# Source scores and row flags written to DRAM by element, and more steps for turned rows, in a six-layer graph network

## The chip, the core and the metric

The kernel runs on one core of a Trainium2 chip. The metric is device time in microseconds (us) of one execution, from launch to end; lower is better. TensorE multiplies matrices into PSUM, VectorE (DVE), ScalarE (ACT) and GpSimd (POOL) work on tiles of 128 partitions, SyncE (SP) issues most DMA transfers. "Dry" or "stopped" means that TensorE has no matmul that it may start.

## The reference

A graph of N = 3327 nodes with 256 features each and a sparse adjacency matrix `adj` passes four attention blocks; the last consists of three layers, so the kernel has six, called 0, 1, 2, 3a, 3b and 3c. Weights, scales and the handling of nodes without neighbours are left out here:

```python
x = layernorm(x + cos_attention(x, adj))      # 0: softmax over Kn @ Qn.T, rows of norm 1
x = layernorm(x + gat(x, adj, W, a))          # 1
x = layernorm(x + qk_attention(x, adj))       # 2: softmax over q @ k.T / 16, values x @ Wv.T
h = x @ W0                                    # 3a, 3b, 3c
for W, a in three_layers:
    h = gat(h, adj, W, a)
x = layernorm(x + h)

def gat(x, adj, W, a):
    h = x @ W
    e = leaky_relu((h @ a[:256]) + (h @ a[256:]).T)   # one source and one target score per node
    att = softmax(where(adj > 0, e, very_negative), axis=1)
    return elu(att @ h)
```

In layer 0 a node without neighbours keeps its features: its flag is whether its sum of weights is zero.

## The kernel before

**Tiles and blocks.** The nodes are padded to 3328, which makes 26 tiles of 128 sources (index j) and 7 blocks of 512 target nodes (index b; block 6, the last, has 256). One step is a triple (layer, block, tile): it makes a tile of unnormalized attention weights `e`, 128 sources by 512 targets, and multiplies it with the 128 by 257 tile of values (the last column is ones and gives the sum of weights), into accumulators `po` in PSUM. The main loop at the end of `gnn_stack` runs over all 6 × 7 × 26 steps; at step s it calls `make(s + 2)`, so weights are made two steps ahead.

**Weights.** In the three GAT layers and layer 1 (`Gat.weights`), ScalarE makes a relu (L599) from the exponential `u` of the source scores of the block, DVE adds and masks it (L607). `u` is loaded from DRAM by `block` (L586, every partition gets the block's row `s_d`, L591 is the exponential; two buffers), in steps 14 and on of the block before. In layer 2 `weights2` takes two matmuls (L506), an exponential (L514) and the mask (L433); layer 0 is alike (L444, L453, L433). Masks are kept in DRAM as bytes (`mask_d`) and fetched a block ahead by L370, 1.66 MB each, at step 8 of a block in program order.

**Products.** Layers 1, 3a, 3b and 3c use plain matmuls (L1163). Layer 2, and blocks 1 to 5 of layer 0, use Strassen's seven products on pairs of tiles (`products`, L704): the sums of the weights (`sums`, L651 to L654) are made by DVE, the sums of the values (`combine`, L625) once per pair when the values are made; they go to DRAM (`t_d`, L636) and are fetched for each block and pair by `fetch_tsum` (L640 to L643, three buffers).

**After a block.** When a block's 26 tiles are accumulated, a generator `finish(L, b, pos)` is appended to a queue, and the main loop advances it by one `yield` per step; at j = 20 of the next block all that is pending is emitted at once. `finish` normalizes (L878 to L882 free the accumulators), turns the rows (`turn`), projects them (`pproj`, L924), applies elu, in layers 0, 1, 2 and 3c the layer norm (L982), writes rows to `x_d` (L994), and for layer 1 turns the result again and makes the values and keys of layer 2 (`pv`, L1011). `NB` is 7, so `b == NB - 2` is block 5, the last full one, and `NB - 1` the last, of 256.

**Turned rows.** `turn` copies the two 16-bit halves of each number into planes (ScalarE, L759), lets SP issue one DMA transposition of them (L762), yields `steps` times, and copies the halves back with DVE (L769, two copies) for the matmul that follows.

**Scores of the next layer.** `Gat.scores` (L533) makes each node's source and target scores on DVE in `self.sd`, one column per tile. `shift` (L548) takes the largest of them, `keys` (L563) the exponentials of the target scores, and `rows(b)` brings the block's source scores to `s_d`: a TensorE transpose (L577, `psr`), a ScalarE copy (L579) and a DMA of four rows of 128 (L580).

**Row flags.** In layer 0 `z0` is 1.0 where a node's sum is below 0.1. A TensorE transpose (L853, `plone`) and a ScalarE copy to bytes (L855) turn it, the mask goes to DRAM (L856), and the flags go into its last row (L857).

**What sets the order.** The program order above is the order of emission. The scheduler of the language then orders the instructions of each engine, except in the first steps, which are ordered by hand. `po` has five PSUM buffers and a block uses three or four, the other PSUM tiles (`ps`, `pproj`, `pv`, `psr`, `plone`) share three, `e` has five buffers. Each engine, SP too, issues in its order, and an instruction that waits holds up those behind it.

Of the kernel before, what the change touches and what calls it, by code (L numbers as in the profile page):

```python
# [8 lines left out]
F32 = mybir.dt.float32  # L9
I32 = mybir.dt.int32  # L10
U8 = mybir.dt.uint8
# [3 lines left out]
ALU = mybir.AluOpType  # L15
# [4 lines left out]
P = 128  # L20
# [13 lines left out]
def gnn_stack(ctx: ExitStack, tc: tile.TileContext, a: dict, N: int, out: bass.AP):  # L34
# [8 lines left out]
    nc = tc.nc  # L43
    NT = (N + P - 1) // P
    NP = NT * P
    NB = (NP + CH - 1) // CH
# [3 lines left out]
    def bw(b):  # L50
        return min(CH, NP - b * CH)

    def tiles_of(b):
        return range(4 * b, min(4 * b + 4, NT))
# [4 lines left out]
    cols = ctx.enter_context(tc.tile_pool(name="cols", bufs=2))  # L59
# [6 lines left out]
    def bank(name):  # L66
        return ps_b.tile([P, CH], F32, tag="pb", name=name)
# [16 lines left out]
    n = 1  # L84
# [9 lines left out]
    ident = const.tile([P, P], F32, name="ident")  # L94
# [12 lines left out]
    s_d = [dram.tile([1, bw(b)], F32, name=f"s_d{b}") for b in range(NB)]  # L107
# [413 lines left out]
    class Gat:  # L521
# [51 lines left out]
        def rows(self, b):  # L573

            n = len(tiles_of(b))
            pr = bank("psr")
            nc.tensor.transpose(pr[:n, :P], self.sd[:, 0, 4 * b : 4 * b + n], ident)  # L577
            r = cols.tile([4, P], F32, tag="srow", name="srow")
            nc.scalar.copy(r[:n], pr[:n, :P])  # L579
            nc.sync.dma_start(s_d[b].rearrange("o (k p) -> (o k) p", p=P), r[:n])  # L580

        def block(self, b):

# [38 lines left out]
    def strassen(L, b):  # L622
        return L.key == "2" or (L.key == "0" and 0 < b < NB - 1)
# [16 lines left out]
    def fetch_tsum(key, b, p):  # L640
        t = work.tile([P, 4 * H + 1], F32, tag="tsum", name="tsums", bufs=3)
        nc.sync.dma_start(t, t_d[key][p])
        tsums[b, p] = t  # L643
# [105 lines left out]
        return z[:, : 2 * q]  # L749


    def turn(x4, n, out, steps=3):

        half = "p k (n t) -> p t k n"
        pl = work.tile([P, 4, 2, D], U16, tag="x4k", name="planes", bufs=2)
        for t in range(2):
            nc.scalar.copy(pl[:, :n, t, :], x4[:, :n, :].bitcast(U16).rearrange(half, t=2)[:, t])  # L759
        yield  # L760
        tr = work.tile([P, 16, P], U16, tag="stage", name="turned", bufs=3)
        nc.sync.dma_start_transpose(  # L762
            out=tr[:, : 4 * n, :], in_=pl[:, :n].rearrange("p k t n -> p (k t n)")
        )
        for _ in range(steps):
            yield
        trv = tr[:, : 4 * n, :].rearrange("p (k t h) i -> p t k h i", t=2, h=2)
        for t in range(2):
            nc.vector.tensor_copy(out(t), trv[:, t])  # L769
        yield  # L770
# [19 lines left out]
    def finish(L, b, pos):  # L790
# [4 lines left out]
        n = len(ts_)  # L795
# [9 lines left out]
        def follow(ks, vals):  # L805

            for k in ks:

                if b == NB - 2:
                    L.late.append((ts_[k], vals[k]))  # L810
                else:
                    L.sum.add(ts_[k], vals[k])
                if L.gat_next is not None:
                    L.gat_next.scores(ts_[k], vals[k])

        if L.key == "0":
            am = anyadj.pop(b)[:, :n]

            if strassen(L, b):
                y4 = work.tile([P, 4, D], F32, tag="x4k", name="y4", bufs=2)  # L820
                z_ = joined(pos, b, y4)
                nc.vector.tensor_scalar(z_, z_, TINY, None, ALU.max)
            else:
                z_ = cols.tile([P, 4], F32, tag="zc", name="zc")
# [14 lines left out]
                ys.append(y)  # L839
            yield  # L840

            z0 = cols.tile([P, 4], F32, tag="z0", name="z0")
            nc.vector.tensor_scalar(z0[:, :n], z_[:, :n], 0.1, None, ALU.is_lt)
            c2 = cols.tile([P, 4], F32, tag="c2", name="c2")
            nc.vector.tensor_scalar(c2[:, :n], am, -1.0, 2.0, ALU.mult, ALU.add)
            for k, t in enumerate(ts_):
# [2 lines left out]
                )  # L849
                if k % 2:  # L850
                    yield
            pl = bank("plone")
            nc.tensor.transpose(pl[:n, :P], z0[:, :n], ident)  # L853
            lone = cols.tile([4, P], U8, tag="lone", name="lone")
            nc.scalar.copy(lone[:n], pl[:n, :P])  # L855
            nc.sync.dma_start(mask_d[b], masks[b][:, : NT * wd])  # L856
            nc.sync.dma_start(  # L857
                mask_d[b][P - 1 : P, (NT - 1) * wd :].rearrange(
                    "o (k p) -> (o k) p", p=P
                ),  # L860
                lone[:n],
            )
            for k in range(n):
                stats(k)
# [2 lines left out]
        else:  # L867
# [15 lines left out]
            if L.key in x_d:  # L883
                x4 = work.tile([P, 4, D], F32, tag="stage", name="x4", bufs=3)
# [9 lines left out]
            if L.key != "2" and not final:  # L894
                pT4 = work.tile([P, 4, 2, P], F32, tag="x4k", name="pT4", bufs=2)
                yield from turn(
                    p4,
                    n,
                    lambda t: pT4[:, :n].bitcast(U16).rearrange(
                        "p k h (i t) -> p t k h i", t=2  # L900
                    )[:, t],
                    5 if b == NB - 2 else 3,
                )
                pTs = {k: pT4[:, k] for k in range(n)}

# [64 lines left out]
        if not L.hidden:  # L970
            v = cols.tile([P, 4], F32, tag="var", name="var")
            nc.vector.tensor_scalar(v[:, :n], st[:, :n, 1], LN_EPS, None, ALU.add)
            r = cols.tile([P, 4], F32, tag="rstd", name="rstd")
            rsqrt(r[:, :n], v[:, :n], n)
            yield
            if L.key in ("1", "3c"):
                o4 = work.tile([P, 4, D], F32, tag="stage", name="o4", bufs=3)
                dsts = [o4[:, k, :] for k in range(n)]
            else:
                dsts = [nxt[t][:, :D] for t in ts_]  # L980
            for k, t in enumerate(ts_):
                nc.vector.tensor_scalar(  # L982
                    dsts[k],
                    ys[k],
                    st[:, k, 0:1],
                    r[:, k : k + 1],
                    ALU.subtract,
                    ALU.mult,
                )
                if L.key == "3c":  # L990
                    q = LASTP if t == NT - 1 else P
                    nc.sync.dma_start(out[t * P : t * P + q, :], dsts[k][:q])
                elif L.key in ("1", "2"):
                    nc.sync.dma_start(x_d["2" if L.key == "1" else "3c"][t], dsts[k])  # L994
                if k == 1:
                    yield
            if L.key == "3c":
                return
            yield
            if L.key == "1":  # L1000
                yield from turn(
                    o4,
                    n,
                    lambda t: FT[b].bitcast(U16).rearrange(
                        "p h (k i t) -> p t k h i", k=4, t=2
                    )[:, t, :n],
                )
                for k, t in enumerate(ts_):
                    pm = bank("pv")
                    for h in range(2):  # L1010
                        nc.tensor.matmul(  # L1011
                            pm[:, :D],
                            FT[b][:, h, k * P : (k + 1) * P],
                            w["v"][:, h, :],
                            start=(h == 0),
                            stop=(h == 1),
                        )
                    nc.vector.tensor_tensor(nxt[t][:, :D], pm[:, :D], w["bv"], ALU.add)
                    if k % 2:
                        yield  # L1020
                        if b < NB - 1:
                            combine("2", t // 2, nxt)
                dsts = [nxt[t][:, :D] for t in ts_]
            for k in range(0, n, 2):
                follow((k, k + 1), dsts)
                yield
# [24 lines left out]
    class Layer:  # L1051
# [6 lines left out]
    layers = [  # L1058
        Layer(0, "0"),
        Layer(1, "1", gat=True),  # L1060
        Layer(2, "2"),
        Layer(3, "3a", gat=True, hidden=True),
        Layer(4, "3b", gat=True, hidden=True),
        Layer(5, "3c", gat=True),
    ]
# [16 lines left out]

    steps = [(L, b, j) for L in layers for b in range(NB) for j in range(NT)]
    made = deque()

    def make(s):
        if s >= len(steps):
            return
        L, b, j = steps[s]
        if strassen(L, b) and j % 2 == 0:  # L1090
            fetch_tsum(L.key, b, j // 2)
        if L.is_gat:
            made.append(L.gat.weights(b, j))
        else:
            made.append((weights0 if L.key == "0" else weights2)(b, j))
            if strassen(L, b) and j % 2:
                e2, e1 = made.pop(), made.pop()
                made.append(None)
                made.append(sums(b, e1, e2))
# [18 lines left out]
    for s in range(LA):  # L1118
        make(s)
# [4 lines left out]
    for s, (L, b, j) in enumerate(steps):  # L1124
# [25 lines left out]
        if j == 0 and first:  # L1150
            load_x(1)
            load_xT(2)
            make(s + LA)
            next(prep[0])
        elif j == 1 and first:
            make(s + LA)
            next(prep[0])
        else:
            make(s + LA)
# [122 lines left out]
```

## Time and profile before

| | |
|---|---|
| median of 3 runs | 2386.36 us (2385.39 to 2390.31) |
| profiled execution | 2386.53 us |
| its span, first to last instruction | 2384.5 us |
| mean granted TensorE clock | 0.996 |
| psr transposes, plone transposes | 28, 7 |
| DMA transpositions (L762) | 34 |
| fetches of sums (tsums) | 156 |
| loads of masks (L370) | 35 |

The span falls into stages, read off the timeline by the first matmuls of each layer. Columns: from and to in us, length, busy us and instructions of each engine, granted clock, mean busy share of the 16 DMA engines, GB/s.

```profile
0.00:110.00 110.00, 101.02 (x415) 76.06 (x416) 78.61 (x266) 65.91 (x179) 3.79 (x71) 0.97 0.61 193
110.00:486.00 376.00, 372.75 (x2366) 299.70 (x2365) 348.74 (x983) 253.04 (x375) 0.45 (x1) 1.00 0.58 182
486.00:825.00 339.00, 336.46 (x1544) 290.86 (x1543) 226.68 (x576) 186.39 (x286) 7.80 (x12) 1.00 0.30 79
825.00:1412.00 587.00, 585.39 (x3205) 421.88 (x3205) 382.93 (x1144) 160.92 (x278) 0.92 (x4) 1.00 0.24 74
1412.00:1732.00 320.00, 318.49 (x1471) 276.30 (x1471) 192.88 (x460) 186.68 (x296) 0.82 (x2) 1.00 0.18 53
1732.00:2052.00 320.00, 318.07 (x1466) 276.24 (x1465) 189.37 (x439) 185.92 (x293) 0.44 (x1) 1.00 0.18 51
2052.00:2366.00 314.00, 313.41 (x1442) 272.79 (x1440) 189.78 (x451) 174.34 (x270) 0.00 (x0) 1.00 0.20 60
2366.00:2385.00 19.00, 3.02 (x13) 1.84 (x12) 6.52 (x27) 2.52 (x6) 0.00 (x0) 0.71 0.07 23
```

The rows are the start, layers 0 to 3c, and the tail; the engines' columns are PE, PEld (TensorE's loads of weights), DVE, ACT and POOL. A matmul of an fp32 tile is two passes; where two follow each other their modelled ends overlap, so the distance from start to start is what TensorE spends on one: 0.434 us for the 257 columns of a tile of values, against a mean duration of 0.381 us per pass on the page.

### The profile page before, as it was taken

What the parts mean: (1) busy time and instruction counts of PE and PEld (TensorE: products, weight loads), DVE (VectorE), ACT (ScalarE), POOL (GpSimd) and SP (SyncE); (2) the same over time, 40 slices, a digit from 0 to 9 for tenths busy, and PEclk for the clock granted to TensorE, in tenths of its full rate; (3) what the DMA queues carried; (4) which work ended last, traced back from release to release, by engine and by line L of the source; (5) the groups of instructions that cost most, each with busy time, mean ns of one, the idle gap of its engine ahead of it and who ended that gap; (6) DMA issues with size and microseconds to landing.
All of it is one profiled execution on the core that took longest, in us unless ns stands there. A gap on an engine that the chain in (4) does not pass through costs nothing.

```text
span 2384.5 us, 33058 instructions
## 1 busy us (share of the span) xinstructions
PE 2348.6 (98%) x11911; PEld 1915.7 (80%) x11911; DVE 1615.5 (68%) x4340; ACT 1215.7 (51%) x1982; POOL 14.2 (1%) x91
## 2 busy tenths in 40 slices
PE   9999999999999999999999999999999999999997
PEld 6687777888888776667767798888888888888886
DVE  7789999866676657567567585556656555655665
ACT  5666666665555422222222255565655555655554
POOL 0000000000000000000000000000000000000000
PEclk9999999999999999999999999999999999999999
DMA  7556555523222322212212221221211111132121
GB/s 230 169 164 193 187 183 185 164 89 87 73 75 64 102 54 91 73 59 87 72 51 73 78 92 47 67 56 31 73 49 43 43 59 50 45 98 69 60 61 27
DMA packets 146233, 212.83 MB, mean 89 GB/s; under 512 B 76062, under 2 KB 100885, under 8 KB 141461
## 3 DMA queue, kind: packets, MB, share of 16 engines
q1 hardware_dynamic: 145796, 210.45, 29.3%
q8 instruction: 94, 1.54, 0.3%
q14 instruction: 71, 0.57, 0.1%
q10 hardware_dynamic: 272, 0.26, 0.1%
HBM read 165.70 MB, written 28.19 MB: 81 GB/s over the span
## 4 chain that ended last, share of the span: by engine, by line
PE 64%; DVE 2%; DMA 1%; ACT 1%; issue 0%; DVEq 0%; POOL 0%; POOLq 0%; SPq 0%; ACTq 0%
PE po L1163 37%; PE ps L506 12%; PE po L704 11%; PE pproj L924 3%; PE pgq L465 1%; DMA turned<-planes 1%; ACT re L599 1%; DMA t_d<-tsum 0%; PE pv L1011 0%; DVE e L607 0%; DVE ejunk L533 0%; DVE pT L769 0%; ACT planes L759 0%; DMA u<-s_d 0%; DVE v L953 0%
## 5 line engine op out<-in xcount | busy, mean ns | idle before, releaser
L1163 PE MATMUL po<-v,e 128*128 128x257 f32 x5720 | 1275.7, 381 | 2.8 <-ACT p L882 2.0
L1163 PEld LDWEIGHTS po<-v,e 128*128 128x128 f32 x5720 | 1083.2, 190 | 178.1 <-issue 14.6
L599 ACT ACTIVATE re<-u,nrh,th 128x512 f32<-128x512 f32 (+1 forms) x728 | 558.8, 783 | 488.6 <-DVE e L607 485.8
L607 DVE SCALAR_TENSOR_TENSOR e<-re,rh,mask 128x512 f32<-128x512 f32 (+1 forms) x728 | 515.1, 711 | 389.5 <-PE po L1163 366.3
L433 DVE SCALAR_TENSOR_TENSOR e<-ex,mask 128x512 f32<-128x512 f32 (+1 forms) x364 | 236.5, 655 | 183.0 <-ACT ex L514 156.7
L506 PE MATMUL ps<-gT,ft 128*128 128x512 f32 (+1 forms) x728 | 307.7, 563 | 0.0
L514 ACT ACTIVATE ex<-ps,off 128x512 f32<-128x512 f32 (+1 forms) x182 | 119.4, 657 | 360.3 <-PE ps L506 332.3
L704 PE MATMUL po<-tsums,ssum 128*128 128x128 f32 (+1 forms) x1794 | 250.1, 275 | 3.0 <-DMA tsums<-t_d 1.6
L704 PEld LDWEIGHTS po<-tsums,ssum 128*128 128x128 f32 x1794 | 224.4, 192 | 5.4 <-DMA tsums<-t_d 2.4
L704 PEld LDWEIGHTS po<-v,e 128*128 128x128 f32 x1196 | 169.7, 191 | 71.6 <-issue 54.3
L506 PEld LDWEIGHTS ps<-gT,ft 128*128 128x128 f32 x728 | 131.9, 190 | 113.6 <-issue 110.7
L704 PE MATMUL po<-v,e 128*128 128x129 f32 x1196 | 183.2, 275 | 0.2 <-DVE e L433 0.2
L453 ACT ACTIVATE ex<-ps 128x512 f32<-128x512 f32 (+1 forms) x182 | 102.9, 565 | 119.3 <-PE ps L444 107.3
L444 PE MATMUL ps<-ft,ft 128*128 128x512 f32 (+1 forms) x312 | 142.9, 566 | 0.8 <-ACT ft L356 0.7
L405 DVE CUSTOM_DVE_ANT_0 acc<-acc,stage 128x1024 uint16<-128x1024 uint16 (+1 forms) x168 | 111.5, 663 | 13.0 <-DMA stage<-in_adj_a 8.3
L704 PE MATMUL po<-v,ssum 128*128 128x128 f32 x598 | 92.3, 275 | 0.0
L704 PE MATMUL po<-tsums,e 128*128 128x128 f32 x598 | 92.2, 275 | 0.0
L397 ACT ACTIVATE mask<-pos 128x1024 uint8<-128x1024 bf16 (+1 forms) x87 | 86.6, 995 | 2.4
L396 ACT ACTIVATE pos<-stage 128x1024 bf16<-128x1024 int32 (+1 forms) x87 | 85.8, 987 | 2.7 <-DVE e L433 2.7
L924 PE MATMUL pproj<-w_l_w,pT 128*128 128x256 f32 x312 | 80.2, 381 | 3.8 <-DVE pT L769 2.2
L704 PEld LDWEIGHTS po<-v,ssum 128*128 128x128 f32 x598 | 79.4, 192 | 0.1
L704 PEld LDWEIGHTS po<-tsums,e 128*128 128x128 f32 x598 | 79.3, 192 | 0.1
(191 smaller groups left out, 1667.9 us busy)
## 6 DMA issues: line engine op xcount, KB each, us to landing
mask<-mask_d SPq DMA_DIRECT2D x30, 1664.0 KB
tsums<-t_d SPq DMA_DIRECT2D x156, 256.5 KB
stage<-in_adj_a SPq DMA_DIRECT2D x78, 512.0 KB
mask_d<-mask SPq DMA_DIRECT2D x6, 1664.0 KB
t_d<-tsum SPq DMA_DIRECT2D x26, 256.5 KB
u<-s_d SPq DMA_DIRECT2D x24, 256.0 KB
mask<-mask_d SPq DMA_DIRECT2D x5, 832.0 KB
v<-in_x SPq DMA_DIRECT2D x26, 128.0 KB
```

Source lines behind the costliest of these rows:

```text
L397: nc.scalar.activation(mask(b, j, 2), t_[:, : 2 * wd], AF.Sign)
L405: nc.vector.tensor_tensor(acc, acc, st[:, h * wd : (h + 1) * wd], ALU.add)
L433: nc.vector.scalar_tensor_tensor(e[:, :wd], t_[:, :wd], 0.0, mask(b, j), ALU.add, ALU.mult)
L444: nc.tensor.matmul(ps[:, :wd], FT[j // 4][:, 0, (j % 4) * P : (j % 4 + 1) * P], FT[b][:, 1, :wd], start=True, stop=True,)
L453: nc.scalar.activation(t_[:, :wd], ps[:, :wd], AF.Exp)
L506: nc.tensor.matmul(ps[:, :wd], FT[j // 4][:, h, (j % 4) * P : (j % 4 + 1) * P], g[:, h, :wd], start=(h == 0), stop=(h == 1),)
L514: nc.scalar.activation(t_[:, :wd], ps[:, :wd], AF.Exp, bias=off, scale=1.0 / D**0.5)
L599: nc.scalar.activation(t_[:, :wd], self.u[b][:, :wd], AF.Relu, bias=self.nrh[:, j : j + 1], scale=self.th[:, j : j + 1],)
L607: nc.vector.scalar_tensor_tensor(e[:, :wd], t_[:, :wd], self.rh[:, j : j + 1], mask(b, j), ALU.add, ALU.mult,)
L704: nc.tensor.matmul(o, x, y, start=(p == 0 and g not in banks[:i]), stop=(p == NT // 2 - 1 and g not in banks[i + 1 :]),)
L924: nc.tensor.matmul(pm[:, :D], pT[:, h, :], w[L.w][:, h, :], start=(h == 0), stop=(h == 1),)
L1163: nc.tensor.matmul(pos[k], es[:, k * P : (k + 1) * P], V[L.i % 2][j], start=(j == 0), stop=(j == NT - 1),)
```

## The change

Four things are changed.

- `rows` issues one DMA that writes the block's columns of `self.sd` to `s_d` with the partition as the running index of DRAM: 128 × 4 elements of four bytes. Transpose and copy are gone.
- In layer 0 DVE writes the flags as bytes, and the DMA into the mask's last row takes them in the same manner, 128 × 4 elements of one byte. Transpose, copy and the fp32 tile are gone.
- `turn` yields 4 times between the transposition and the copies in place of 3; the projection's turn 7 in place of 5 for block 5; the turn of layer 1's output 6 in place of 3 for block 5.
- `make` fetches the sums of a pair one pair earlier, except for pair 12 of layer 2's first block.

```diff
@@ rows @@
             n = len(tiles_of(b))
-            pr = bank("psr")
-            nc.tensor.transpose(pr[:n, :P], self.sd[:, 0, 4 * b : 4 * b + n], ident)
-            r = cols.tile([4, P], F32, tag="srow", name="srow")
-            nc.scalar.copy(r[:n], pr[:n, :P])
-            nc.sync.dma_start(s_d[b].rearrange("o (k p) -> (o k) p", p=P), r[:n])
+            nc.sync.dma_start(
+                s_d[b].rearrange("o (k p) -> (o p) k", p=P),
+                self.sd[:, 0, 4 * b : 4 * b + n],
+            )
@@ turn @@
-    def turn(x4, n, out, steps=3):
+    def turn(x4, n, out, steps=4):
@@ finish, layer 0 @@
-            z0 = cols.tile([P, 4], F32, tag="z0", name="z0")
-            nc.vector.tensor_scalar(z0[:, :n], z_[:, :n], 0.1, None, ALU.is_lt)
+            lone = cols.tile([P, 4], U8, tag="lone", name="lone")
+            nc.vector.tensor_scalar(lone[:, :n], z_[:, :n], 0.1, None, ALU.is_lt)
...
-            pl = bank("plone")
-            nc.tensor.transpose(pl[:n, :P], z0[:, :n], ident)
-            lone = cols.tile([4, P], U8, tag="lone", name="lone")
-            nc.scalar.copy(lone[:n], pl[:n, :P])
             nc.sync.dma_start(mask_d[b], masks[b][:, : NT * wd])
             nc.sync.dma_start(
                 mask_d[b][P - 1 : P, (NT - 1) * wd :].rearrange(
-                    "o (k p) -> (o k) p", p=P
+                    "o (k p) -> (o p) k", p=P
                 ),
-                lone[:n],
+                lone[:, :n],
             )
@@ finish, projection's turn @@
-                    5 if b == NB - 2 else 3,
+                    7 if b == NB - 2 else 4,
@@ finish, turn of layer 1's output @@
+                    6 if b == NB - 2 else 4,
@@ make @@
-        if strassen(L, b) and j % 2 == 0:
-            fetch_tsum(L.key, b, j // 2)
+        if j % 2 == 0:
+            for n in (s, s + 2):
+                if n < len(steps) and not (n > s and steps[n] == (layers[2], 0, NT - 2)):
+                    if strassen(*steps[n][:2]) and n not in fetched:
+                        fetch_tsum(steps[n][0].key, steps[n][1], steps[n][2] // 2)
+                        fetched.add(n)
```

More of the change, by code (lines that the diff above doesn't have):

```diff
@@ L1084, in gnn_stack @@
     made = deque()
+    fetched = set()
     def make(s):
```

## The prediction

> **What bounds the kernel now.** I read the page's busy times first, then the chain, then TensorE's list of waits, then the timeline at the boundaries of the layers.
>
> ```profile
> span 2384.5 us, 33058 instructions
> ...
> PE 2348.6 (98%) x11911; PEld 1915.7 (80%) x11911; DVE 1615.5 (68%) x4340; ACT 1215.7 (51%) x1982; POOL 14.2 (1%) x91
> ...
> q1 hardware_dynamic: 145796, 210.45, 29.3%
> ...
> PE po L1163 37%; PE ps L506 12%; PE po L704 11%; PE pproj L924 3%; PE pgq L465 1%; DMA turned<-planes 1%; ACT re L599 1%; DMA t_d<-tsum 0%; PE pv L1011 0%; DVE e L607 0%; DVE ejunk L533 0%; DVE pT L769 0%; ACT planes L759 0%; DMA u<-s_d 0%; DVE v L953 0%
> ```
>
> TensorE is the bound: busy 98% of the span and, by line, nearly all of the chain. So only two kinds of edit move the time: work taken off TensorE, and a longer or shorter stop of TensorE. All SP transfers share one queue, q1, with room on average (29.3%).
>
> The list of waits says what TensorE's stops are (total us, times, longest):
>
> ```profile
> PE pproj L924 <- DVE pT L769: 3.1, 6, 0.7
> ...
> PE po L1163 <- ACT p L882: 2.0, 2, 1.3
> PE po L704 <- DMA tsums<-t_d: 1.6, 1, 1.6
> ...
> PE psr L577 <- DVE sd L533: 1.1, 1, 1.1
> ...
> PE pv L1011 <- DVE ft L769: 1.0, 1, 1.0
> ...
> PE pn L488 <- DVE g L485: 0.5, 1, 0.5
> ```
>
> These are the stops that the change can touch; together they are under 10 us. The tile table of psr counts the transposes, and the timeline shows the end of layer 1 (start, duration, engine, line) and the one long stop early in the kernel:
>
> ```profile
> L577 PE MATMUL psr<-ident,sd x28: 269/272/273, 151.7 to 2070.6; 128*4 128x128 f32 x24, 128*2 128x128 f32 x4
> ```
> ```profile
> 816.54 1.94 SPq L762 DMA_TRANSPOSE turned<-planes  x1
> ...
> 816.80 4.58 PE L1163 MATMUL po<-v,e 128*128 128x257 f32 x20
> ...
> 819.16 0.36 SPq L370 DMA_DIRECT2D mask<-mask_d  x1
> ...
> 820.87 1.36 DVE L769 COPY ft<-turned 128x1024 uint16<-128x1024 uint16 x2 [0.51 <-DMA turned<-planes]
> ...
> 822.37 3.69 PE L1011 MATMUL pv<-w_l_wvt,ft 128*128 128x256 f32 x16 [0.99 <-DVE ft L769]
> ```
> ```profile
> 101.91 1.12 PE L352 MATMUL pqkT<-ident,qk 128*128 128x128 f32 x4 [3.31 <-DVE qk L346]
> ```
> ```profile
> 100.00:101.00 1.00, 0.00 (x0) 0.00 (x0) 0.90 (x5) 0.00 (x0) 0.00 (x0) 0.80 0.87 332
> 101.00:102.00 1.00, 0.09 (x1) 0.10 (x1) 0.93 (x6) 0.43 (x2) 0.00 (x0) 0.50 0.44 158
> ```
>
> The last two lines are slices of 1 us; the number after ACT's and POOL's is the granted clock. After a stop of 3.31 us it falls to 0.50. The mean clocks of the slices 95 to 102 (0.90) and 102 to 110 us (0.66) give 1.4 and 5.4 us at half rate, 6.8 in all, which costs half of that, 3.4 us.
>
> **What the Trainium skill says.** "TensorE: Matmul & The Clock Gate" (Part 1: The HAM clock gate) says that TensorE falls to half rate after an idle window of about 3.4 us, a free-running one, and needs about 3.4 us of work to come back; the trace agrees in kind (3.31 us, then 6.8 us at half). "DMA: Bandwidth & Descriptors" (Rules for kernel authors) says that a strided last dimension lowers to one descriptor per element; no such write is in the trace of before. The same page (Bandwidth) has 10.5 ns of busy time per small packet; the trace's 4-byte and 16-byte packets took 9 ns. Its section on queues and rings says that each ring is consumed in order, which makes what stands ahead in SP's queue matter.
>
> **The change part by part**, on the profiled execution, 2386.53 us (span 2384.5 and 2.03 around it), which lies 0.17 above the median, 2386.36.
>
> *Transposes.* 28 psr and 7 plone leave TensorE. A row says 272 ns, but with its overlap the next matmul starts 0.11 us after (psr at 463.36, next at 463.46): 35 × 0.11 = 3.9 us. In 110–486 us, where 13 of them stand, DVE is busy for 349 of 376 us and might swallow their 1.4; elsewhere nothing does. I take −3.9, range −2.5 to −3.9. ScalarE's 35 copies (28 × 256, 7 × 239 ns, 8.8 us) cost nothing now: ScalarE is at 51%. The psr stop at 463.36 (1.1 idle) goes, but DVE's scores, 8 L533 rows, hold up the next weights there: −0.5 (0 to −1.1).
>
> *Element-wise writes.* 28 of 512 (4 of them 256) 4-byte elements, and 7 of one-byte ones, all on q1. Low: 512/16 × 9 ns = 0.3 us. High: read-modify-write at ten times that, 3 us a write. s_d is read a block or a layer later, mask_d a layer later, so either is hidden. In layer 2 the load u<-s_d and a sum's fetch stand behind such a write; a pair of steps is 6.56 us and fetches run up to two pairs ahead, so 3 us fits. I take 0, up to +1. If that cover were gone, each of the writes beyond it would show in full.
>
> *Sums one pair earlier.* SP still waits for the buffer (three of them) that the products L704 release; it did so at 138 fetches, 491 us in all, so the order on SP hardly moves: 0. The exempted pair 12 of layer 2's first block has the 1.6 us stop on tsums; it stays.
>
> *More steps for turned rows.* From L762 to the first copy takes 4.3 us (816.54 to 820.87) to 5.3 (742.72 to 748.02), the two copies 1.36. Ordinary turns get one step more, four matmuls of 0.434 us, 1.7: their stops (0.32 at 749.43, 0.28 at 1612.81; 0.48 and 0.45 by the starts of the matmuls) go: −0.9. The turns of the last-but-one block (about 0.75 each, four times) get two steps more for the copies, but in the built order the first projection stands where it stood: 0 (0 to −1.5).
>
> *Ends of 3a and 3b.* The two steps more push shift, L548, from the 18th to the 20th tile of the last block and so the second exp of u (L591, it waits for a DMA, 0.67 us) behind the copies L882 that free the accumulators. L882 then comes earlier; the stops of 0.63 and 1.32 (0.80 and 1.49 by starts) mostly go: −1.8 (0 to −2.3). Late next is the weights' work on DVE, which has 2.5 us.
>
> *End of layer 1.* Here steps are added at the wrong place. Block 5's output turn gets 3 steps more and its projection turn 2, but at j=20 of the next block all that is pending is emitted at once. In the built order the normalization L982 comes behind the last weights e (L607 of tile 25), and then planes, L762, copies, pv L1011. In SP's queue the next mask's load L370 (1.66 MB, which waits for the last e) and four rows of x (L994) now stand ahead of L762, where L370 stood behind it before. Let T be the end of tile 20's matmuls. Ten matmuls × 0.434 = 4.3 us are left, so TensorE is dry at T+4.3. DVE has o4 at about T+2.3, ScalarE's two planes (1.99) end at T+4.3: the transposition is only then issued. It takes 4.3 to 5.3, copies 1.36, and up to some us for what is left of the mask (8 packets an engine × 498 ns = 4.0 us, most of it done by then) and x (1.5 us). Stop: 4.6 + 1.4 + 1.0 = 7.0 us, ends 5.7 and 9.6. Before, the stops at pv and pn were 1.7 (1.16 and 0.68 by starts, less rounding): +5.3 (4.0 to 7.9). A stop beyond 3.31 us brings the half clock: +3.4, as measured at 101 us (1.7 to 3.4). Nothing in layer 2 makes this up: pv stands ahead of ps L506 on TensorE. What follows the turn moves with it, the sums' t_d writes L636 among it, but their pairs are fetched some 60 us into layer 2 (ten pairs of 6.56 us).
>
> Sum: −3.9 −0.5 −0.9 −1.8 = −7.1; +5.3 +3.4 = +8.7; net +1.6, so 2388.1 on the profile, 2388.0 on the median. Ends of this case: gains of 4.0 to 7.6, losses of 5.7 to 11.3, so −1.9 to +7.3; the middle of that with opposite ends rarely meeting is 2384.5 to 2392.
>
> **The rivals.**
> *The stop at the end of layer 1 stays hidden* (0.16): the chip runs ScalarE's planes early enough that L762 is issued 3 us sooner, as DVE's idle gaps in that stretch allow. The stop is then 3.3 or less and keeps the clock: +1.5, net −5.6, 2380.8. For it: the built order fixes only the sequence, not the times. Against: L982 behind the last e.
> *Slower: the mask's load delays the transposition* (0.36). If its packets take the 926 ns of their 90th percentile, 7.4 us a load, 3.7 are still ahead of the turn when it is issued, and x's 1.5: stop 4.8 + 1.36 + 5.2 = 11.4, +9.7, clock +3.4, gains −7.1: +6.0, 2392.4. It decides from a stop of about 10.2 us with all gains, or 7 with gains of 3.9. For it: ring order; against: at 29% the queue drains.
> *Element writes show* (0.03 of the slower cases): at 0.3 us a packet, 9.6 us a write, 3 beyond the 6.6 of a pair in layer 2's seven: +21, 2409.
> *The change doesn't do what it says*: for the sums' fetches this I take as likely (0 above); for the transposes it can't be.
>
> **How the numbers follow.** Within 0.2% means ±4.8 us (2381.6 to 2391.1), about what a measurement of this kernel tells from no change. Forecast case 0.48: nearly all of it lies within. Hidden stop 0.16: faster. Mask 0.33 and element writes 0.03: slower, the latter far out. So faster 0.17 with the forecast's low tail, same 0.46, slower 0.37. The time is the forecast's, 2388.0; the range takes in the hidden stop to 2380 and the mask's delay with its upper end, 2396.5.
>
> **What would show it.** 5983 TensorE instructions in place of 6018, no psr or plone. At the end of layer 1 pv L1011 with an idle of 6 to 10 us <-DVE ft L769, and a slice of clock 0.5 after it. No stop at L924 in ordinary blocks, still 0.7 at the last-but-one's. po L1163 <- ACT p L882 under 0.5 in all. The tsums' 1.6 unchanged. I am wrong if pv's idle is under 3 us, or if u<-s_d or tsums stop TensorE in layer 2.

## The result and the profile after

The changed kernel takes 2534.94 us (median of 5 runs, 2531.90 to 2535.43) against 2386.81 us of the kernel before beside it (5 runs): a ratio of 1.0616, 95% interval 1.0601 to 1.0632, or +148 us. The prediction, 2388.0 us with a range to 2396.5, is far off.

The page of the changed kernel, lines as those shown of before:

```profile
span 2529.7 us, 32926 instructions
...
PE 2372.8 (94%) x11876; PEld 1937.5 (77%) x11876; DVE 1613.8 (64%) x4340; ACT 1204.4 (48%) x1947; POOL 12.9 (1%) x91
...
PEclk9988988888999999999999999999999999999999
...
q1 hardware_dynamic: 162736, 210.45, 35.5%
```

The span grew by 145.2 us. TensorE's idle time went from 35.9 (2384.5 - 2348.6) to 156.9 us, +121.0; its busy time grew by 24.2 although 35 transposes are gone. The clock's row says why: in seven of the slices 3 to 10 the granted clock is 0.8, since TensorE comes out of its long stops at half rate (the last column but two in the slices below). All but two of TensorE's new stops over 2 us lie in the first 640 us, in layer 0 and at the start of layer 1.

The list of TensorE's waits of the changed kernel (total us, times, longest):

```profile
PE po L703 <- DMA tsums<-t_d: 45.2, 6, 15.4
PE po L703 <- issue: 30.4, 4, 11.9
PE po L1166 <- DVE e L433: 27.5, 2, 20.1
PE pv L1007 <- DVE ft L768: 9.2, 1, 9.2
...
PE pproj L919 <- DVE pT L768: 4.4, 5, 1.7
...
PE po L1166 <- ACT p L877: 1.5, 3, 0.6
```

The fourth line is the stop that was predicted. The first three were not. In the first and the third, layer 0 waits for loads from DRAM: of the sums directly (four of the six times; the other two, 4.0 and 1.1 us, are in layer 2), and of adjacency stages, for which DVE waits ahead of e. For the four stops of the second line the profile names no releaser; they end 16 to 28 us after a write of flags was issued. The DMA engines show what happens in slices around one of the first line's stops. Columns as in the table of stages: granted clock, DMA share and GB/s at the end.

```profile
214.00:217.00 3.00, 3.00 (x26) 2.78 (x25) 3.00 (x11) 2.71 (x5) 0.00 (x0) 1.00 0.66 168
217.00:222.00 5.00, 5.00 (x36) 4.04 (x35) 4.81 (x14) 4.73 (x9) 0.00 (x0) 1.00 1.14 41
222.00:227.00 5.00, 5.00 (x36) 4.04 (x35) 5.00 (x19) 3.20 (x4) 0.00 (x0) 1.00 1.04 38
227.00:232.00 5.00, 2.58 (x12) 1.43 (x11) 5.00 (x19) 1.19 (x2) 0.00 (x0) 1.00 0.99 23
232.00:237.00 5.00, 0.00 (x0) 0.00 (x0) 3.45 (x15) 0.00 (x0) 0.00 (x0) 0.67 0.87 19
237.00:243.00 6.00, 0.00 (x0) 0.00 (x0) 0.00 (x0) 0.00 (x0) 0.00 (x0) 0.50 0.69 52
243.00:247.00 4.00, 1.99 (x9) 2.02 (x10) 0.69 (x1) 2.11 (x2) 0.00 (x0) 0.50 0.89 317
```

The flags of a block are written at 214.13 us (the timeline of SP and of TensorE):

```profile
214.13 0.37 SPq L852 DMA_DIRECT2D mask_d<-lone  x1
```
```profile
228.75 0.83 PE L703 MATMUL po<-v,e 128*128 128x129 f32 x6
245.01 2.04 PE L703 MATMUL po<-tsums,ssum 128*128 128x128 f32 x8 [15.43 <-DMA tsums<-t_d]
```

From 217 to 237 us the DMA engines are busy for about all of their time and move 19 to 41 GB/s, where layer 0 of before, between 201 and 211 us, moves about 160 at a share of 0.54: they are held, not loaded. TensorE lives on what was fetched, until 229.6, and then stops for 15.43 us. Single packets say the same: the 4096-byte packets of the adjacency stages take 0.16 us in the ordinary case, up to 11 us here. The 512 packets of one byte show 9 ns each, all within 1.6 us. A packet's own busy time hides here what it does to the others.

The time that a transfer takes can be read from the events on its semaphore, from SP's issue to the last one seen:

```
transfer                                   before        after
flags of a block, 512 (last block 256)     1.1 to 2.8    28 to 31 (full blocks; one has too few events)
source scores of a block, in 3a and 3b     1.1 to 2.0    8.3 to 11.4
loads of sums (before: 150 to 300 us;      2.6 to 5.4    20.9 to 27.8
  after: the three issued at 217 to 227)
```

The predicted stop, at the end of layer 1 in the changed kernel (timeline, and one slice behind it):

```profile
948.76 0.33 SPq L370 DMA_DIRECT2D mask<-mask_d  x1
949.16 2.35 SPq L989 DMA_DIRECT2D x_d<-o  x4
...
952.40 5.81 SPq L761 DMA_TRANSPOSE turned<-planes  x1
...
960.23 1.37 DVE L768 COPY ft<-turned 128x1024 uint16<-128x1024 uint16 x2 [7.37 <-DMA turned<-planes]
...
961.66 6.62 PE L1007 MATMUL pv<-w_l_wvt,ft 128*128 128x256 f32 x16 [9.19 <-DVE ft L768]
```
```profile
964.00:966.00 2.00, 2.00 (x6) 1.64 (x5) 0.98 (x4) 0.00 (x0) 0.00 (x0) 0.50 0.00 0
```

The order is the one worked out: mask, four rows of x, then the transposition. From its issue to the first copy it took 7.8 us in place of 4.3, and TensorE went on at half clock.

### The profile page after: what moved, and what is told of

It reads as the page before. It is cut to its first block, busy times and chain, and to the rows that moved or that the text cites. A ratio compares the mean times of both kernels' runs of the same rounds, so it can differ in the third digit from the quotient of the medians.

```text
span 2529.7 us, 32926 instructions
## 1 busy us (share of the span) xinstructions
PE 2372.8 (94%) x11876; PEld 1937.5 (77%) x11876; DVE 1613.8 (64%) x4340; ACT 1204.4 (48%) x1947; POOL 12.9 (1%) x91
## 4 chain that ended last, share of the span: by engine, by line
PE 82%; DMA 10%; DVE 4%; ACT 2%; issue 1%; another core or an unknown queue 1%; DVEq 0%; POOL 0%; POOLq 0%; SPq 0%; ACTq 0%
PE po L1166 45%; PE po L703 16%; PE ps L506 11%; DMA tsums<-t_d 4%; PE pproj L919 3%; PE ps L444 3%; DMA stage<-in_adj_a 3%; DMA stage<-in_adj_z 2%; PE pv L1007 1%; DMA turned<-planes 1%; DVE acc L405 1%; PE pgq L465 1%; DVE e L433 1%; ACT re L598 1%
## 5 line engine op out<-in xcount | busy, mean ns | idle before, releaser
L703 PE MATMUL po<-tsums,ssum 128*128 128x128 f32 (+1 forms) x1794 | 259.6, 282 | 54.3 <-DMA tsums<-t_d 45.2
L703 PEld LDWEIGHTS po<-tsums,ssum 128*128 128x128 f32 x1794 | 232.9, 198 | 57.8 <-issue 28.3
L506 PEld LDWEIGHTS ps<-gT,ft 128*128 128x128 f32 x728 | 132.9, 192 | 114.7 <-issue 111.4
L444 PE MATMUL ps<-ft,ft 128*128 128x512 f32 (+1 forms) x312 | 145.2, 577 | 0.8 <-ACT ft L356 0.7
```

Source lines behind the costliest of these rows:

```text
L444: nc.tensor.matmul(ps[:, :wd], FT[j // 4][:, 0, (j % 4) * P : (j % 4 + 1) * P], FT[b][:, 1, :wd], start=True, stop=True,)
L506: nc.tensor.matmul(ps[:, :wd], FT[j // 4][:, h, (j % 4) * P : (j % 4 + 1) * P], g[:, h, :wd], start=(h == 0), stop=(h == 1),)
L703: nc.tensor.matmul(o, x, y, start=(p == 0 and g not in banks[:i]), stop=(p == NT // 2 - 1 and g not in banks[i + 1 :]),)
```

## The experiments

Theory A: a write of many elements that lie side by side in DRAM holds all transfers, some 28 us for bytes and 9 us for four-byte elements, and TensorE runs dry in it. Theory B: the earlier fetches of the sums crowd buffers and queue. Each run is compared with runs of the kernel before on its own chip; differences are of medians.

### The four parts apart

**flags**: the row flags alone.

```diff
+lone = cols.tile([P, 4], U8, tag="lone", name="lone")
+nc.vector.tensor_scalar(lone[:, :n], z_[:, :n], 0.1, None, ALU.is_lt)
-z0 = cols.tile([P, 4], F32, tag="z0", name="z0")
-nc.vector.tensor_scalar(z0[:, :n], z_[:, :n], 0.1, None, ALU.is_lt)
...
-pl = bank("plone")
-nc.tensor.transpose(pl[:n, :P], z0[:, :n], ident)
-lone = cols.tile([4, P], U8, tag="lone", name="lone")
-nc.scalar.copy(lone[:n], pl[:n, :P])
...
-"o (k p) -> (o k) p"  ...  lone[:n]
+"o (k p) -> (o p) k"  ...  lone[:, :n]
```

> The kernel before with the row flags alone written by element (seven writes of 512 or 256 single bytes). Theory A (each such write holds every transfer behind it for some 28 us, and TensorE runs dry in it): +100 to +130 us, seven stops of 5 to 20 us in layer 0 and at the start of layer 1, each within 30 us after such a write. Theory B (it is the earlier fetches of the sums that crowd the buffers and the queue): within 3 us of before, slightly faster by seven transposes, 0.8 us.

2497.64 against 2384.85 us, +112.8 (ratio 1.0475, 1.0459 to 1.0491). TensorE's waits of this kernel:

```profile
PE po L704 <- DMA tsums<-t_d: 59.3, 5, 14.8
PE po L1159 <- DVE e L433: 18.6, 1, 18.6
```

Seven writes of at most half a kilobyte carry three quarters of the whole loss. Each is followed by a stop (the first by two) whose end lies 29 to 32 us behind the issue of the write. These stops come to 97.9 us, and TensorE's busy time grew by 14.7, although seven transposes are gone: together 112.6.

**scores**: the source scores alone (`rows` as in the change).

> The kernel before with the source scores alone written by element (28 writes of 512 or 256 four-byte elements). Theory A: such a write holds the queue for about 9 us, less than the stock of fetched tiles lasts: in layer 0, where transfers are dense, some stops, +5 to +20 us; nothing in 3a to 3c. Theory B: within 4 us of before, -3 us by the 28 transposes.

2406.95 us, +22.1 (1.0098, 1.0081 to 1.0115). More than expected, and at one place where no loss was expected:

```profile
PE po L1162 <- ACT p L881: 9.7, 2, 5.8
PE po L1162 <- DVE e L433: 7.9, 2, 7.0
PE po L703 <- DMA tsums<-t_d: 3.3, 2, 2.7
```

The second and third lines are in layers 0 and 2. The first is at the ends of 3a and 3b (3.9 and 5.8 us). SP's and ScalarE's timeline there:

```profile
2053.57 0.38 SPq L576 DMA_DIRECT2D s_d<-sd  x1
2056.53 0.32 SPq L585 DMA_DIRECT2D u<-s_d  x1
```
```profile
2064.64 0.72 ACT L590 ACTIVATE u<-u,ub 128x512 f32<-128x512 f32 x1 [5.05 <-DMA u<-s_d]
2065.26 2.91 ACT L598 ACTIVATE re<-u,nrh,th 128x512 f32<-128x512 f32 x4
2068.08 0.81 ACT L881 ACTIVATE p<-po,ri 128x256 f32<-128x256 f32 x2
```

The load of u, issued 3 us after the write, lands 8 us later; ScalarE waits with its exponential for 5.05 us, and behind it in ScalarE's order stand the relus and the copies L881 that free TensorE's accumulators.

**turns** and **turnsfetch**: the steps alone, and the steps with the earlier fetches (both as in the change).

> The kernel before with the additional steps of the turns alone. Both theories: pv at the end of layer 1 stops for 7 to 9 us in place of 1.0, TensorE's clock halves for some 6.8 us after it, and 2 to 3 us come back at the ordinary turns and at the ends of 3a and 3b: +5 to +10 us.

> The kernel before with the additional steps and the earlier fetches of sums, both kinds of writes as before. Theory A: equal to the run with the steps alone within 2 us, since the fetches wait for the same three buffers. Theory B: +100 us or more.

2393.38 us, +8.5 (1.0040, 1.0025 to 1.0055), and 2393.27 us, +8.4 (1.0038, 1.0023 to 1.0053). Theory B falls: the fetches alone change nothing. The first wait of the kernel with the steps is the one predicted:

```profile
PE pv L1012 <- DVE ft L769: 9.2, 1, 9.2
```

**flagsback**: the changed kernel with only the flags put back.

```diff
-lone = cols.tile([P, 4], U8, tag="lone", name="lone")
-nc.vector.tensor_scalar(lone[:, :n], z_[:, :n], 0.1, None, ALU.is_lt)
+z0 = cols.tile([P, 4], F32, tag="z0", name="z0")
+nc.vector.tensor_scalar(z0[:, :n], z_[:, :n], 0.1, None, ALU.is_lt)
...
+pl = bank("plone")
+nc.tensor.transpose(pl[:n, :P], z0[:, :n], ident)
+lone = cols.tile([4, P], U8, tag="lone", name="lone")
+nc.scalar.copy(lone[:n], pl[:n, :P])
...
-"o (k p) -> (o p) k"  ...  lone[:, :n]
+"o (k p) -> (o k) p"  ...  lone[:n]
```

> The changed kernel with the row flags alone put back to transpose, copy and four rows. If the parts only add: the scores' +22 and the steps' +8.4, +30 us. If the additional steps hide the scores' writes at the ends of 3a and 3b (the exponential of u then comes after the accumulators are freed), where the scores alone stopped TensorE for 3.9 and 5.8 us: +18 to +22 us.

2407.28 against 2386.46 us, +20.8 (1.0089, 1.0074 to 1.0105), not +30: the steps hide what the scores' writes did at the ends of 3a and 3b, where TensorE's waits for L881 fell from 9.7 to 1.2 us. ScalarE there in this kernel:

```profile
2064.93 0.71 ACT L590 ACTIVATE u<-u,ub 128x512 f32<-128x512 f32 x1
2065.67 4.35 ACT L598 ACTIVATE re<-u,nrh,th 128x512 f32<-128x512 f32 x6
2069.93 0.45 ACT L881 ACTIVATE p<-po,ri 128x256 f32<-128x256 f32 x1
```

One exponential of u stands there, the other comes at 2074.50, behind L881, which so waits for no transfer.

### What is slow in such a write

**probe**: the kernel before, and in each block of 3a and 3b one more write of 512 elements, from a few columns of e, into DRAM that nothing reads.

```diff
+if L.key in ("3a", "3b") and j == 10:
+    nc.vector.tensor_copy(probe, es[:, : 4 * m])
+    nc.sync.dma_start(
+        spare[i][:, 0:m].rearrange("(k p) m -> p k m", p=P),
+        probe.rearrange("p (k m) -> p k m", m=m),
+    )
```

> The kernel before with one more write of 512 elements in each of the 14 blocks of 3a and 3b, where transfers are few; nothing reads them. They differ in element size and in the distance of the elements in DRAM. Time from issue to the last landing. If the cost comes from elements that share a small piece of DRAM (A1): single bytes side by side about 28 us, bytes 64 or 512 bytes apart under 4 us, two-byte elements side by side 15 us, four-byte ones 9 us, four-byte ones 64 bytes apart under 4 us. If every small write costs the same (A2): bytes 28 us and four-byte elements 9 us at any distance.

Issue to last event, us:

```
bytes of an element   distance in DRAM   us
1                     1                  29.1, 29.3
1                     2                  14.9
2                     2                  15.2
1                     4                   9.5
4                     4                   9.3, 8.4
4                     8                   3.2
16                    16                  2.7
1                     64                  1.8
2                     64                  2.0
4                     64                  1.8
1                     512                 1.9
4                     512                 3.4
```

The distance decides, not the size of an element and not the number of packets (512 in each): a byte every four bytes takes as long as four bytes every four, and a byte every two as long as two every two. Each row has one write, or two where two times stand. With half the elements, 256 in the last block of 512, a write side by side was hardly shorter (25.7 against 28 to 31 us for the bytes of the run dense below, 8.3 to 9.5 against 8.7 to 11.4 for the scores written after layer 0 in the changed kernel). So the time is not one per element; it fits elements that share a small piece of DRAM being written one after the other, pieces beside each other. How large a piece is, the runs don't tell; but it isn't 512 bytes, since at 64 bytes apart eight elements share as much and the write takes no longer than at 512 apart. The page "DMA: Bandwidth & Descriptors" of the Trainium skill (Specifications) says that transfers under 512 B are read-modify-writes; that would make writes to one piece wait for each other, but it gives no price, and no run here shows that memory is read for such a write. What happens in the memory stays open.

Few transfers are no sure cover. The kernel with these 14 writes took 2400.37 us in its only run, against 2385.30 of before. TensorE has two new stops over 4 us in it, 5.0 us ending at 1460.28 and 4.5 us ending at 1774.79. Each follows one of the two writes of bytes side by side (issued at 1419.72 and 1746.57), and no other write has such a stop behind it, although the DMA share of 3a and 3b is 0.18 before. What handed the delay on there was not followed up.

**dense** and **spread**: the kernel before with its own flags, and one more write of them into spare DRAM, side by side or 64 bytes apart.

```diff
+flag = cols.tile([P, 4], U8, tag="flag", name="flag")
+nc.vector.tensor_scalar(flag[:, :n], z_[:, :n], 0.1, None, ALU.is_lt)
+nc.sync.dma_start(
+    spare[b][:, 0:1].rearrange("(k p) o -> p (k o)", p=P)[:, :n], flag[:, :n]
+)                       # spare[b]: [512, 1] bytes, or [512, 64]
```

> The kernel before, and beside its own flags in layer 0 one more write of the flags, by element, into DRAM that nothing reads, the bytes side by side. If the write itself, by holding what stands behind it, is the cost (A1 and A2): +100 to +120 us, as the flags alone had. If it were the place in the mask's row, or a reader that waits for it: within 5 us of before.

> The same with the bytes 64 bytes apart in DRAM, the same number of packets. A1 (shared pieces of DRAM): within 8 us of before. A2 (each small write): +100 to +120 us.

Side by side: 2499.99 against 2385.30 us, +114.7 (1.0475, 1.0459 to 1.0491). 64 bytes apart: 2386.95, +1.7 (1.0009, 1.0000 to 1.0017). The packets, the queue and the place in the program are the same: nearly the whole cost comes from the elements' being neighbours in DRAM, and neither the mask's row nor a reader of it is needed for it.

**denseact**: the write side by side, from ScalarE's queue (`nc.scalar.dma_start`).

> The kernel before with the additional flags, bytes side by side, issued by ScalarE into its own queue in place of SP's. If what holds the others is the order of SP's queue: within 8 us of before. If the 16 DMA engines themselves are held, whatever queue a transfer came by: +90 to +120 us, as from SP's queue (+113).

2504.50 against 2386.46 us, +118.0 (1.0496, 1.0482 to 1.0510). TensorE's first waits:

```profile
PE po L705 <- DMA tsums<-t_d: 53.8, 4, 19.2
PE po L1170 <- DVE e L434: 21.4, 1, 21.4
```

The sums' loads are in SP's queue and still wait, and SP itself waits for the write to land only once, for 2.8 us. So it isn't the order of one queue, nor SP waiting for the write: the DMA engines are held.

### The end of layer 1, and a better version

**turnsp7**: all steps but those of the output's turn of block 5 (3 as before; the projection's turn stays at 7, as in the change).

> The kernel before with the additional steps, but the turn of layer 1's output of block 5 left at 3; the projection's turn at 7. If the output's three steps are what puts its transposition behind the last weights: pv's stop back at 1 to 2 us, -2 to -3 us to before. If the projection's two steps do it alone: pv's stop 7 to 9 us as with all steps, +8 us.

2393.54 us, +7.1 (1.0039, 1.0025 to 1.0053), and

```profile
PE pv L1012 <- DVE ft L769: 8.8, 1, 8.8
```

The two steps of the projection's turn alone put the output behind the last weights (the next run takes them away, and the stop goes). The three of the output's turn add nothing that shows.

**best**: the projection's turn of block 5 at 5 in layer 1 and 7 in the other layers, the output's at 3, the others at 4; no other part.

```diff
-def turn(x4, n, out, steps=3):
+def turn(x4, n, out, steps=4):
-5 if b == NB - 2 else 3,
+(5 if L.key == "1" else 7) if b == NB - 2 else 4,
+3 if b == NB - 2 else 4,        # output of layer 1
```

> The kernel before with the additional steps of the turns only where they don't delay the end of layer 1: default and ordinary turns 4, the projection's turn of block 5 still 5 in layer 1 and 7 in 3a and 3b, the turn of layer 1's output still 3 for block 5. Expected from the steps of the prediction: -0.9 us at the ordinary turns, -1.8 us at the ends of 3a and 3b, the stop at pv as before: -2 to -3 us.

2384.15 against 2385.30 us, -1.2 (0.9993, 0.9985 to 1.0001): less than the expected -2 to -3, and the interval takes in no change. The stop at pv is back at 1.0 us:

```profile
822.35 1.97 PE L1012 MATMUL pv<-w_l_wvt,ft 128*128 128x256 f32 x8 [1.00 <-DVE ft L769]
```

**best2**: that, and scores by element from blocks of 3a and 3b only.

```diff
-L.gat_next.rows(b)
+L.gat_next.rows(b, L.hidden)      # L.hidden: 3a, 3b; by element if true
```

> The version with the steps that don't delay the end of layer 1, and the scores written by element only by blocks of 3a and 3b, where transfers are few and the writes lie ahead of nothing that is due within 9 us: 14 transposes x 0.11 = 1.5 us less than that version, 3 to 4 us less than before, if the writes of some 9 us stay hidden there; slower than before by 2 to 8 us if the load of u that stands behind the last of them is late.

2384.14 against 2386.46 us, -2.3 (0.9988, 0.9981 to 0.9994): faster than the kernel before by 0.1%, less than expected. The writes take 7.9 to 10.8 us there, and TensorE doesn't wait for them; its waits for the accumulators are all short:

```profile
PE po L1170 <- ACT p L888: 1.2, 2, 0.6
```

## Why the prediction was wrong

**Element-wise writes: the step that failed.** It read "High: read-modify-write at ten times that, 3 us a write ... I take 0, up to +1". The flags take 28 to 31 us and the scores 8.3 to 11.4 (12.8 beside layer 0's loads), and alone they cost +112.8 and +22.1.

The price came from the busy time of small packets of before, 9 ns. By the trace these are 512 packets of 16 bytes, which are four loads, and 9780 of four bytes, about 16 for each of its 608 transfers, none of which has elements of four bytes: no write of single elements to DRAM is among them. The new packets do show 9 ns, and their cost is in others' packets. The bound above was a multiple of that price with nothing to support it.

"Either is hidden" was argued from who reads the rows, and the readers do no harm: twice in layer 2 SP waits for such a write to land before it may load u (8.7 and 8.5 us), and TensorE doesn't stop. But what stands in the same DMA engines, which are well used in layer 0 (share 0.58), was not asked. TensorE had some 15 us of fetched tiles; 28 us is beyond that, 9 us only in places.

The rival "element writes show" had the kind of mechanism, but got its 9.6 us a write from 0.3 us a packet, where the packets show 9 ns; that it is near what the scores take is luck. It put the loss into all seven writes of layer 2, where one stopped TensorE (4.0 us, up to 1542.87), left out the flags, and had a chance of 0.03.

**End of layer 1: right in mechanism and place, a little small in size.** Predicted +5.3 for the stop (to 7.0 from 1.7) and +3.4 for the clock. Measured: 9.63 (9.19 at pv and 0.44 still at pn) from 1.51 (0.99 + 0.52), so +8.1, and half clock from 961.66 to about 967.6, which costs 3.0: +11.1 against +8.7, just within the ends of 5.7 to 11.3. The mis-sized term is the transposition behind mask and rows of x, 7.8 us from issue to copy against 5.6 (4.6 + 1.0). The cause was given to both turns; the projection's two steps do it alone (turnsp7).

**Steps elsewhere.** The stops of the two ordinary turns are gone in the run with the steps, but the one of layer 1's block 5 grew from 0.71 to 1.10, so the waits of L924 for turned rows fell only from 3.1 to 2.8 us, where -0.9 was written. L882's waits fell from 2.0 to 1.0 us, about half of the -1.8. All in all the steps cost +8.5 where -0.9 -1.8 +8.7 = +6.0 was written.

**Sums one pair earlier:** 0, as predicted (turnsfetch less turns, -0.1). The stop at the exempted pair stays at 0.8 to 1.6 us.

**Transposes:** gone (11876 matmuls in place of 11911); their -3.9 can't be read on its own in any run. best2 against best, -2.3 and -1.2 to their own runs of before, is in keeping with 1.5 for 14 of them, and doesn't show it.

**The sum of the gains.** The ends written for it, 4.0 to 7.6, are not those of the terms: their own ranges add up to 3.4 and 9.7. Nothing in the outcome hangs on it.

**The sum by runs:** flags 112.8, all else 20.8 (flagsback): 133.6 of 148.1. The 14.5 left belong to no run, and their cause is open. By the profiles TensorE's idle time grew by 9.6 us more than in the two runs together (121.0 against 94.5 + 16.9), its busy time by 5.3 (24.2 against 14.7 + 4.2). No single stop carries it: the stop of 7.4 us behind the scores' write at 576.30 is in scores and flagsback too, with 7.0 and 6.9. Both kinds of writes without the other parts, and the flags together with the steps or the fetches, were not run.

## What to carry to other kernels

Before turning an on-chip transpose into an element-wise write to DRAM, ask how many of its elements lie side by side: 512 bytes in a row held the other transfers for some 28 us, and the same 512, spread 64 bytes apart, were done in 2. Such a cost didn't show in the packet's own time but in that of the others, so its cover is the stock of what is already fetched, in each stage, and not the slack of who reads it. And where pending work is emitted all at once at a fixed step, more steps in one part can throw a later part behind the end of the layer.

## What was not expected of the hardware

- Small neighbouring writes hold the transfers of SP's queue whether they are issued from SP's queue or from ScalarE's (+114.7 and +118.0 us), with 9 ns shown per packet.
- The time follows the distance: about 29, 15, 9, 3.2 and 1.8 us at 1, 2, 4, 8 and 64 bytes, for 512 elements each, and half the elements took hardly less.
- Stops of TensorE of some 15 us cost more than themselves: its busy time grew by 24.2 us at half clock although work was taken away.
